# A perceiver layer on one core: the key-side queries of the later pairs turned once and dealt out by ScalarE, the second pair's loads held back, and the first products in another order

## The chip, the core and the metric

The kernel runs on one core of one Trainium2 chip. The metric is the device time of one execution in microseconds; the median of three runs before the change is 295.79 us (295.11 to 296.79). The profile is of one further execution, whose own time is given below.

## What is computed

A block takes x (8 sequences of 64 rows, 512 wide) and a context of 8 x 1601 rows, 512 wide. Three steps each add to x: attention of x on the context, an attention with a sigmoid in place of the softmax, and a feed-forward layer of 8 experts of which each row takes one. All of it is in float32. The change lies in the first step, whose reference is:

```python
qp = einsum('bsd,de->bse', layernorm(x), Wq) + bq
kp = einsum('bsd,de->bse', ctx, Wk) + bk
vp = einsum('bsd,de->bse', ctx, Wv) + bv
logits = einsum('bqe,bke->bqk', qp, kp) / sqrt(512)
x = x + einsum('bqk,bke->bqe', softmax(logits), vp)
```

## The kernel before

The keys are never made. The logits are (q Wk^T) ctx^T plus a term that is the same along a row, and the attention output is (p ctx) Wv. So each row's query is multiplied by Wk^T once ("key product", `keyed`, L308), scored against the raw context, and the context itself is summed with the probabilities.

The 512 rows of x are four tiles of 128, which are four pairs p = 0 to 3 of sequences. Each pair's context, two sequences of 1601 rows, comes in three groups of 512 rows and a tail of 65 (`load_group`, L205), one slab per group and sequence. There are twelve slabs in all; the weights use them too, and a load has to wait until a slab's last reader is done.

For the scores the context must lie with its 512 columns along the partitions. VectorE turns it in 32x32 blocks (`turn_group`, L231), which leaves four 32-row bands a = 0 to 3 of context rows; a T block holds one quarter q of the columns for one sequence and is made of three pieces and a tail. There are five T buffers, which the exponentials L share. A score matmul (`scores`, L363) takes 32 rows of R and 32 rows of T, so R must hold each 32 values of a query in all four bands. Before the change that is done in three steps: GpSimd writes q Wk^T four times over (`spread`, L335: four copies), TensorE turns the sixteen 128x128 blocks of that (`fill_queries`, L354: "turns" in what follows are such transposes, done as matmuls with an identity), and ScalarE copies them into R in four copies of 128x512. R has one buffer.

The stages of the first step, by pair: scores (`scores`, [...]four quarters), softmax (`softmax`, L376: maxima on VectorE, five exponentials on ScalarE), turns of the exponentials with a copy to SBUF on ScalarE (`chances`, L409, giving pt), sums over the context (`attend`, L418), division (`divided`, L430, giving acs), a turn of acs (`turned_sums`, L435) and the product with Wv (`project`, L440), which goes to x one pair later. Between them stand the later steps of earlier pairs: norm and turn of x, the products with aWq, aWk and aWv, alignment, sums, output (aWo), and for the pair before that the gate of the experts (`gate_parts` L690, whose copy `shares` at L700 TensorE needs for `gate`, L703).

TensorE's order is the order of the program text throughout (a manual schedule, L253). In the opening stretch VectorE and ScalarE follow the text too (L296, L876); elsewhere a scheduler orders them. [...] SyncE issues the loads of x, weights and context; GpSimd issues seven loads of constants (L886 to L892: bv, lnw, lnb, gwT, gq, gk, bo) and later blank rows and scattered rows. Instructions that are marked `keep_in_program_order` stay in the text's order on their engine.

The opening runs like this: normalise tile 0, turn it, multiply by Wq (`project_q`, L279), key product of tile 0 (L877); then turn tiles 1 to 3 (L878), multiply them by Wq (L881), turn the spread key product of tile 0 into R (L883), and start the scores. Key products of tiles 1 to 3 stand together after the first pair's softmax (L928).

Of the kernel before, what the change touches and what calls it, by code (L numbers as in the profile page):

```python
# [17 lines left out]
P = 128  # L18
B, S, D = 8, 64, 512
SK = 1601  # L20
NT = B * S // P
DC = D // P
# [14 lines left out]
def perceiver_kernel(ctx: ExitStack, tc: tile.TileContext, out: bass.AP, t: dict):  # L37
    nc = tc.nc
# [12 lines left out]
    def slab(name):  # L51
        return slabs.tile([P, DC, D], F32, tag="slab", name=name)

    def row(name):
        return rowp.tile([P, D], F32, tag="row", name=name)
# [19 lines left out]
    def load_w(name):  # L75
        w = slab(f"w_{name}")
        nc.sync.dma_start(out=w, in_=t[name])
        return w
# [23 lines left out]
    def load_b(name, n, c=None):  # L102
        if c is None:
            c = const.tile([P, n], F32, tag=name, name=f"c_{name}")
        tc.keep_in_program_order(
            nc.gpsimd.dma_start(out=c, in_=t[name].partition_broadcast(P))
        )
        return c
# [65 lines left out]
    def transposed(src, name):  # L174
        tp = bank4(f"t_{name}")
        for dc in range(DC):
            nc.tensor.transpose(tp[:, dc, :], src[:, dc * P : (dc + 1) * P], ident)
        return tp

    def projected(srcT, w, name, between=None):  # L180
        ps = bank(f"p_{name}")
        for dc in range(DC):
            if dc == DC // 2 and between is not None:
                between()
            nc.tensor.matmul(  # L185
                ps, lhsT=srcT[:, dc, :], rhs=w[:, dc, :],
                start=(dc == 0), stop=(dc == DC - 1),
            )
        return ps
# [29 lines left out]
    cxs = {}  # L219
    for g in (3, 0, 1, 2):  # L220
        cxs[0, g] = load_group(0, g)
    wv = load_w("xWv")


    NB = D // 32
    WIDTH = (416, 416, 385, 384)
# [1 line left out]
    def block_tile(p, q, b2):  # L228
        return blkp.tile([P, 4, 416], F32, tag="blk", name=f"T_{p}_{q}_{b2}")
# [41 lines left out]
    def turn_x(i, xn):  # L271
        tp = transposed(xn, f"xn{i}")
        step = 2 if i == 0 else DC
        for dc in range(0, DC, step):
            nc.scalar.copy(  # L275
                xnT[:, dc : dc + step, i * P : (i + 1) * P], tp[:, dc : dc + step, :]
            )
# [27 lines left out]

    qks = {}

    def keyed(p):  # L308

        cols = slice(p * P, (p + 1) * P)  # L310
        ps = projected(qpT[:, :, cols], wkT, f"qk{p}")
        qks[p] = row(f"qk{p}")
        nc.scalar.copy(qks[p], ps)  # L313

    def biased():

        ps = bank("qb")
        for ec in range(DC):
            for p in range(NT):
                nc.tensor.matmul(  # L320
                    ps[32 * p : 32 * p + 32, :P],
                    lhsT=bk[:, ec : ec + 1].to_broadcast([P, 32]),
                    rhs=qpT[:, ec, p * P : (p + 1) * P],
                    start=(ec == 0), stop=(ec == DC - 1),
                )
        qbT = rowp.tile([P, P], F32, tag="row", name="qbT")
        nc.scalar.copy(qbT, ps[:, :P])
        return qbT
# [6 lines left out]
    def spread(p):  # L335

        qk = qks.pop(p)
        got = []
        for b0 in range(0, NB, 4):
            q4 = rowp.tile([P, 4, 4, 32], F32, tag="row", name=f"q4_{p}_{b0}")  # L340
            nc.gpsimd.tensor_copy(  # L341
                q4,
                qk[:, 32 * b0 : 32 * b0 + 128].rearrange(
                    "p (b d) -> p b d", d=32
                ).unsqueeze(2).to_broadcast([P, 4, 4, 32]),
            )
            got.append(q4)
        return got
# [5 lines left out]
    def fill_queries(p, R, q4s, half):  # L354
        for b0 in range(8 * half, 8 * half + 8, 4):
            tp = bank4(f"rt_{p}_{b0}")
            for j in range(4):
                nc.tensor.transpose(
                    tp[:, j, :], q4s[b0 // 4][:, j, :, :].rearrange("p a d -> p (a d)"), ident
                )  # L360
            nc.scalar.copy(R[:, b0 : b0 + 4, :], tp)

    def scores(p, q, R, sc, Ts, js=range(4)):  # L363
        for j in js:
# [53 lines left out]
    def attend(p, g, pt, ac):  # L418
        cx = cxs.pop((p, g))
        nch, m = extent(g)  # L420
        for j in range(nch):
            for b2 in range(2):
                r = b2 * S
                rhs = cx[b2][:, j, :] if g < 3 else cx[b2][:m, :]
                nc.tensor.matmul(  # L425
                    ac[r : r + S, :], lhsT=pt[:m, j, r : r + S], rhs=rhs,
                    start=(g == 0 and j == 0), stop=(g == 3),
                )

    def divided(p, ac, r):  # L430
        acs = row(f"acs_{p}")
        nc.vector.tensor_scalar(acs, ac, r, None, ALU.mult)
        return acs
# [431 lines left out]
    def load_pair(p):  # L865
        for g in range(4):
            cxs[p, g] = load_group(p, g)

    def quarter(p, q):
        return [blocks(p, q, b2) for b2 in range(2)]  # L870

    def do(*steps):
        for f, i in steps:
            f(i)

    with tc.manual_schedule(engines={mybir.EngineType.Activation}):  # L876
        keyed(0)  # L877
        for i in range(1, NT):  # L878
            turn_x(i, later[i - 1])
    q4s = spread(0)  # L880
    project_q(1, NT - 1, [bank(f"qp1_{ec}") for ec in range(DC)])  # L881
    R = queries(0)
    fill_queries(0, R, q4s, 0)  # L883
    fill_queries(0, R, q4s, 1)
    qbT = biased()
    bv = load_b("xbv", D, row("c_xbv"))  # L886
    lnw = load_late("lnw", [P, DC])
    lnb = load_late("lnb", [P, DC])
# [3 lines left out]
    bo = load_b("bo", D)  # L892
    for i in range(NT):
        nc.gpsimd.tensor_tensor(xs[i], xs[i], bv, ALU.add)
    Ts = [first[0, 0], first[0, 1]]
    load_pair(1)
    awq, awk, awv, awo = (load_w(n) for n in ("aWq", "aWk", "aWv", "aWo"))
    for p in range(NT):
        i = p - 2
        if 0 < p < NT - 1:  # L900
            q4s = spread(p + 1)
        sc = [bank(f"sc_{p}_{a}") for a in range(4)]
        for q in range(4):
            if p == 0 and q == 0:
                nTs = [first[1, 0], first[1, 1]]
            elif p == 0 and q == 1:
                nTs = [first[2, 0], blocks(0, 2, 1)]
            else:
                nTs = quarter(p, q + 1) if q < 3 else None
            if i >= 0 and q == 3:  # L910
                scores(p, q, R, sc, Ts, range(3))
                do((back, i))
                scores(p, q, R, sc, Ts, (3,))
            else:
                scores(p, q, R, sc, Ts)
            Ts = nTs
            if p == 0 and q == 0:
                unturned(qbT)
            if i >= 0 and q < 3:
                do(((split, align, sums)[q], i))  # L920
        L, r = softmax(p, sc)
        pts = []

        def chance():
            pts.append(chances(p, len(pts), L))

        if p == 0:
            for k in range(1, NT):  # L928
                keyed(k)
                if k == 1:  # L930
                    q4s = spread(1)
            tables()
        else:
            do((at_turn, p - 1))
            if i >= 0:
                do((output, i))
        if p + 1 < NT:
            R = queries(p + 1)
            if p == 0:
                chance()  # L940
                fill_queries(1, R, q4s, 0)
            elif p == 1:
                fill_queries(2, R, q4s, 0)
                do((at_out, 0))
                chance()
            else:
                do((at_out, p - 1))
                fill_queries(p + 1, R, q4s, 0)
                chance()
            fill_queries(p + 1, R, q4s, 1)  # L950
        else:
            at_out(p - 1, chance)
        if 0 < p < NT - 1:
            load_pair(p + 1)
        if p == 1:
            blank_rows()
        ac = bank(f"ac_{p}")
        if i >= 0:
            do((face, i))
        for g in range(4):  # L960
            if g < 3:
                chance()
            if p > 0 and g == 3:
                do((turn, p - 1))
            if i >= 0 and g == 1:
                do((gated, i))
            attend(p, g, pts[g], ac)
            if p > 0 and g == 0:
                do((norm, p - 1))
            if i >= 0 and g == 0:  # L970
                do((logits, i))
            if i >= 0 and g == 1:
                do((routed, i))
        tile_of[p]["acs"] = divided(p, ac, r)
        if 0 < p < NT - 1:
            do((unit_q, p - 1))
            Ts = quarter(p + 1, 0)
            do((unit_k, p - 1), (gates, p - 1), (values, p - 1))
        elif p == 0:
            Ts = quarter(1, 0)  # L980


    gu, dn = load_experts()
# [218 lines left out]
```

## Time and profile before

| | before |
|---|---|
| median of 3 runs | 295.79 us |
| time of the profiled execution | 295.09 us |
| span of its instructions | 293.4 us |
| granted TensorE clock, mean | 0.998 |
| TensorE busy | 279.1 us (95%) |
| VectorE busy | 159.6 us (54%) |
| ScalarE busy | 93.2 us (32%) |
| GpSimd busy | 63.9 us (22%) |
| moved by DMA | 57.71 MB, 197 GB/s over the span |

The span runs from the first to the last instruction of the program; the time also holds some 1.7 us around it. In lines of the profile, PE is TensorE's matmuls, PEld its weight loads, DVE VectorE, ACT ScalarE, POOL GpSimd and SPq SyncE's queue. A line of a timeline gives start and duration in us, then engine, source line, operation, what it writes and reads, and how many such instructions are merged; in square brackets stands the idle time before it and what ended that. A line of the waits gives who waited for whom, and the total, the number and the longest in us. Busy time of TensorE counts matmuls that run into each other, so a short wait between two of them may not show as idle; it then shows in the waits of PEld.

### The profile page before, as it was taken

The page shows a single profiled execution, that of the slowest core. Times are in us where ns is not written, and L with a number is a line of the kernel's source. Part 1 is how long each engine was busy: PE and PEld are TensorE (multiplying, and loading weights), DVE is VectorE, ACT ScalarE, POOL GpSimd, SP SyncE. Part 2 cuts the span into 40 slices and gives each one's busy share as a digit, 9 for nine tenths or more (in the row PEclk, how much of TensorE's full clock was granted, in tenths as well). Part 3 has the DMA queues.
Part 4 walks back from the last instruction along what each step waited for, and adds up shares of the span by engine and source line. Part 5 has one row for each costly group of instructions (what it writes and reads, how often), then busy time and mean ns, then how long its engine had stood idle before and what let it go on. Part 6 is the DMA issues. An engine that isn't in the chain of part 4 may idle for free. (4 is left out here: it accounts for less than half of the span.)

```text
span 293.4 us, 6477 instructions
## 1 busy us (share of the span) xinstructions
PE 279.1 (95%) x2661; PEld 138.3 (47%) x2661; DVE 159.6 (54%) x414; ACT 93.2 (32%) x203; POOL 63.9 (22%) x110
## 2 busy tenths in 40 slices
PE   5689999999999999999999999999999999999991
PEld 5555664633554244655534465534454455343320
DVE  2554487336853477956667794453372466374140
ACT  3221403620037131326714143652425434130110
POOL 4055400600081002500220310022050032413301
PEclk9999999999999999999999999999999999999999
DMA  6999980189974993000199401959991200523401
GB/s 185 348 414 396 344 330 1 32 347 416 386 275 163 359 417 122 4 3 0 29 395 369 142 2 26 370 188 329 376 376 61 74 0 2 158 92 117 175 3 43
DMA packets 20288, 57.71 MB, mean 197 GB/s; under 512 B 2274, under 2 KB 10514, under 8 KB 16544
## 3 DMA queue, kind: packets, MB, share of 16 engines
q1 hardware_dynamic: 17568, 50.37, 47.5%
q0 software_dynamic: 2400, 6.89, 6.3%
q8 instruction: 23, 0.38, 0.5%
q14 instruction: 9, 0.07, 0.1%
q10 hardware_dynamic: 288, 0.00, 0.1%
HBM read 50.94 MB, written 6.84 MB: 197 GB/s over the span
## 5 line engine op out<-in xcount | busy, mean ns | idle before, releaser
L233 DVE STREAM_TRANSPOSE T<-cx 128x512 f32<-128x512 f32 x96 | 61.9, 681 | 25.1 <-DMA cx<-in_ctx_dram 19.4
L369 PE MATMUL sc<-T,R 32*64 32x416 f32 (+2 forms) x1024 | 49.9, 501 | 0.1
L425 PE MATMUL ac<-cx,pt 128*64 128x512 f32 x192 | 43.8, 599 | 0.0
L369 PEld LDWEIGHTS sc<-T,R 32*64 32x64 f32 x1024 | 26.5, 131 | 17.6 <-issue 6.8
L425 PEld LDWEIGHTS ac<-cx,pt 128*64 128x64 f32 x192 | 12.7, 136 | 22.1 <-issue 21.2
L1010 PE MATMUL gu<-wgu,xeT 128*32 128x512 f32 x192 | 22.9, 597 | 0.0
L501 POOL TENSOR_TENSOR gm_k<-qn_k,c_gk 128x512 f32<-128x512 f32 x4 | 5.1, 1284 | 61.4 <-DVE qn_k L496 61.4
L185 PE MATMUL p_qk<-w_xWkT,qpT 128*128 128x512 f32 x32 | 14.2, 598 | 2.9 <-DMA w_xWkT<-in_xWkT_dram 2.9
L464 POOL TENSOR_TENSOR x<-x,c_bo 128x512 f32<-128x512 f32 x4 | 5.1, 1268 | 53.6 <-DVE xh L463 53.6
L341 POOL COPY q<-qk 128x512 f32<-128x512 f32 x16 | 9.0, 615 | 34.0 <-ACT qk L313 34.0
L284 PE MATMUL qp<-xnT,w_xWq 128*128 128x128 f32 (+1 forms) x64 | 14.4, 384 | 1.3 <-ACT xnT L275 1.3
L185 PE MATMUL p_q<-w_aWq,xhT 128*128 128x512 f32 x32 | 14.8, 605 | 0.1
L185 PE MATMUL p_k<-w_aWk,xhT 128*128 128x512 f32 x32 | 14.7, 595 | 0.0
L185 PE MATMUL p_po<-w_xWv,acT 128*128 128x512 f32 x32 | 14.7, 595 | 0.0
L380 DVE TENSOR_REDUCE mx<-sc 128x1 f32<-128x416 f32 (+2 forms) x16 | 8.1, 567 | 11.9 <-PE sc L369 11.9
L185 PE MATMUL p_o<-w_aWo,cT 128*128 128x512 f32 x32 | 14.5, 596 | 0.0
L185 PE MATMUL p_v<-w_aWv,xvT 128*128 128x512 f32 x32 | 14.4, 592 | 0.0
L415 ACT COPY pt<-pp 128x512 f32<-128x512 f32 (+1 forms) x16 | 8.2, 515 | 17.5 <-PE pp L413 15.8
L284 PEld LDWEIGHTS qp<-xnT,w_xWq 128*128 128x128 f32 x64 | 9.7, 191 | 5.7 <-ACT xnT L275 1.8
L1045 PE MATMUL y<-wd,hT 128*32 128x512 f32 x96 | 11.5, 596 | 0.6 <-DVE hT L1037 0.6
L185 PEld LDWEIGHTS p_qk<-w_xWkT,qpT 128*128 128x128 f32 x32 | 5.8, 190 | 10.5 <-issue 7.4
L1020 DVE TENSOR_TENSOR h<-gu,h 128x256 f32<-128x256 f32 x6 | 2.5, 424 | 14.0 <-ACT h L1019 14.0
(198 smaller groups left out, 387.6 us busy)
## 6 DMA issues: line engine op xcount, KB each, us to landing
cx<-in_ctx_dram SPq DMA_DIRECT2D x24, 1024.0 KB, 10.1
wgu<-in_wgT_dram SPq DMA_DIRECT2D x8, 512.0 KB, 9.2
wgu<-in_wuT_dram SPq DMA_DIRECT2D x8, 512.0 KB, 10.0
wd<-in_wdT_dram SPq DMA_DIRECT2D x8, 512.0 KB, 8.4
rd<-blank POOLq DMA_DIRECT2D x6, 258.0 KB, 4.8
in<-rd SPq DMA_DIRECT2D x6, 258.0 KB, 5.0
xd<-blank POOLq DMA_DIRECT2D x6, 256.0 KB, 4.8
in<-xd SPq DMA_DIRECT2D x6, 256.0 KB, 7.2
```

The source lines that it names most:

```text
L185: nc.tensor.matmul(ps, lhsT=srcT[:, dc, :], rhs=w[:, dc, :], start=(dc == 0), stop=(dc == DC - 1),)
L233: nc.vector.transpose(T[:, :, 128 * g : 128 * g + 128].rearrange("p b (c k) -> p b c k", k=32), cxs[p, g][b2][:, :, 128 * q : 128 * q + 12 ...
L284: nc.tensor.matmul(ps[ec][:, : n * P], lhsT=wq[:, dc, ec * P : (ec + 1) * P], rhs=xnT[:, dc, cols], start=(dc == 0), stop=(dc == DC - 1),)
L341: nc.gpsimd.tensor_copy(q4, qk[:, 32 * b0 : 32 * b0 + 128].rearrange("p (b d) -> p b d", d=32).unsqueeze(2).to_broadcast([P, 4, 4, 32]),)
L369: nc.tensor.matmul(sc[a][r : r + S, : WIDTH[a]], lhsT=R[32 * a : 32 * a + 32, b, r : r + S], rhs=Ts[b2][32 * a : 32 * a + 32, j, : WIDTH[a ...
L380: nc.vector.tensor_reduce(mx[:, a : a + 1], sc[a][:, : WIDTH[a]], AX.X, ALU.max)
L415: nc.scalar.copy(pt[:m, :nch, :], tp[:m, :nch, :])
L425: nc.tensor.matmul(ac[r : r + S, :], lhsT=pt[:m, j, r : r + S], rhs=rhs, start=(g == 0 and j == 0), stop=(g == 3),)
L464: nc.gpsimd.tensor_tensor(xs[i], xs[i], bo, ALU.add)
L501: nc.gpsimd.tensor_tensor(heads(gm), heads(qn), gb.unsqueeze(1).to_broadcast([P, H, HD]), ALU.mult)
L1010: nc.tensor.matmul(ps[c, :], lhsT=xTs[k][:, dc, c], rhs=ffw[e][0][:, dc, :], start=(dc == 0), stop=(dc == DC - 1),)
L1045: nc.tensor.matmul(y[c, :], lhsT=hT[:, ic, c], rhs=ffw[e][1][:, ic, :], start=(ic == 0), stop=(ic == IC - 1),)
```

## The change

It has four parts.

- The first products. The key product of tile 0 takes a `between` argument: after two of its four matmuls the turns of tiles 1 to 3 are put, with ScalarE's copies of them; its other two matmuls follow, and the copy of the product follows on ScalarE.
- Held loads. Two slabs are written by a one-column copy on GpSimd that reads the last column of qpT, ahead of the seven constant loads on that queue; the second pair's first loads can have those slabs only after that. The load of Wv (`wv`) goes from ahead of the second pair's loads on SyncE's queue to behind them. As only ten slabs are in use by then, the second pair's first four loads get the slabs of Wq, xnT and the two held ones; its last two get those of the first pair's first group. Before, they waited for those of WkT and qpT, which now go to aWo and the third pair's first load.
- Turned and dealt. For pairs 1 to 3, `turn_queries` turns q Wk^T itself in four blocks, and `deal_queries` copies from PSUM to R in 16 copies of 32 partitions x 512, four for each band, put between the sums over the context. `spread` and `fill_queries` stay for pair 0 alone. The key product of tile 3 goes to the second pair's turn, after that of acs.
- Orders by hand. VectorE follows the text from the first pair's softmax to the second pair's second quarter: T blocks of quarters 0 and 1 of the second pair by group, the third group's two for quarter 0 ahead of `divided`, the two for quarter 1 behind it. ScalarE follows the text from each softmax to the last deal.

The diff, with context lines cut:

```diff
-    wv = load_w("xWv")
...
-    def keyed(p):
+    def keyed(p, between=None):
...
-        ps = projected(qpT[:, :, cols], wkT, f"qk{p}")
+        ps = projected(qpT[:, :, cols], wkT, f"qk{p}", between)
...
+    def turn_queries(p):
+
+        return transposed(qks.pop(p), f"rt_{p}")
+
+    def deal_queries(R, tp, a):
+
+        for j in range(4):
+            nc.scalar.copy(R[32 * a : 32 * a + 32, j::4, :], tp[32 * j : 32 * j + 32, :, :])
...
-        keyed(0)
-        for i in range(1, NT):
-            turn_x(i, later[i - 1])
+        def turn_later():
+            for i in range(1, NT):
+                turn_x(i, later[i - 1])
+
+        keyed(0, turn_later)
...
+    for k in range(2):
+        tc.keep_in_program_order(
+            nc.gpsimd.tensor_copy(slab(f"held{k}")[:, 0, 0:1], qpT[:, DC - 1, NT * P - 1 :])
+        )
     bv = load_b("xbv", D, row("c_xbv"))
...
+    def turn_second(g, qs=range(2)):
+        for b2 in range(2):
+            for q in qs:
+                turn_group(second[q, b2], 1, q, b2, g)
+
     Ts = [first[0, 0], first[0, 1]]
     load_pair(1)
+    wv = load_w("xWv")
     awq, awk, awv, awo = (load_w(n) for n in ("aWq", "aWk", "aWv", "aWo"))
     for p in range(NT):
         i = p - 2
-        if 0 < p < NT - 1:
-            q4s = spread(p + 1)
...
+            elif p == 1 and q == 0:
+                nTs = [second[1, 0], second[1, 1]]
...
+                if p == 1 and q == 1:
+                    turns.__exit__(None, None, None)
...
+        if p > 0:
+            do((at_turn, p - 1))
         L, r = softmax(p, sc)
         pts = []
+        if p == 0:
+            turns = tc.manual_schedule(engines={mybir.EngineType.DVE})
+            turns.__enter__()
+            second = {(q, b2): block_tile(1, q, b2) for q in range(2) for b2 in range(2)}
+            for g in (0, 3, 1):
+                turn_second(g)
+        acts = ExitStack()
+        if p < NT - 1:
+            acts.enter_context(tc.manual_schedule(engines={mybir.EngineType.Activation}))
...
         if p == 0:
             for k in range(1, NT):
-                keyed(k)
-                if k == 1:
-                    q4s = spread(1)
+                if k < NT - 1:
+                    keyed(k)
+            turned_qk = turn_queries(1)
+            R = queries(1)
             tables()
         else:
-            do((at_turn, p - 1))
             if i >= 0:
                 do((output, i))
-        if p + 1 < NT:
+        if p == 0:
+            chance()
+        elif p + 1 < NT:
             R = queries(p + 1)
-            if p == 0:
-                chance()
-                fill_queries(1, R, q4s, 0)
-            elif p == 1:
-                fill_queries(2, R, q4s, 0)
-                do((at_out, 0))
-                chance()
-            else:
-                do((at_out, p - 1))
-                fill_queries(p + 1, R, q4s, 0)
-                chance()
-            fill_queries(p + 1, R, q4s, 1)
+            if p == 1:
+                keyed(NT - 1)
+            do((at_out, p - 1))
+            chance()
+            turned_qk = turn_queries(p + 1)
...
             attend(p, g, pts[g], ac)
+            if p < NT - 1 and g < 3:
+                deal_queries(R, turned_qk, g)
+                if p == 0 and g == 2:
+                    deal_queries(R, turned_qk, 3)
...
+        if p == 0:
+            turn_second(2, (0,))
         tile_of[p]["acs"] = divided(p, ac, r)
+        if p == 0:
+            turn_second(2, (1,))
         if 0 < p < NT - 1:
             do((unit_q, p - 1))
+            deal_queries(R, turned_qk, 3)
+        acts.close()
+        if 0 < p < NT - 1:
             Ts = quarter(p + 1, 0)
             do((unit_k, p - 1), (gates, p - 1), (values, p - 1))
         elif p == 0:
-            Ts = quarter(1, 0)
+            Ts = [second[0, 0], second[0, 1]]
```

## The prediction

> **What bounds the kernel now.** I read the page's first part, then the timelines of TensorE, VectorE and ScalarE stage by stage, then the waits of two stretches.
>
> ```profile
> PE 279.1 (95%) x2661; PEld 138.3 (47%) x2661; DVE 159.6 (54%) x414; ACT 93.2 (32%) x203; POOL 63.9 (22%) x110
> ```
> TensorE is busy in 279.1 of 293.4 us. It takes its work in program order, so a microsecond is saved only where one of its instructions goes or one of its waits goes. The chain of waits holds only the last store and tells nothing here. The waits from 10 to 37 us:
>
> ```profile
> PE p_qk L185 <- DMA w_xWkT<-in_xWkT_dram: 2.9, 1, 2.9
> ...
> PE qp L284 <- ACT xnT L275: 0.8, 1, 0.8
> PEld sc L369 <- DVE T L233: 0.8, 1, 0.8
> ```
> Three stops of TensorE: for wkT, for the copies of turned x, and for the first scores' second context block. From 44 to 85 us another, inside a stretch that the page counts as busy, because matmuls run into each other:
>
> ```profile
> PEld sc L369 <- DVE T L240: 0.9, 2, 0.7
> ```
> The timelines of TensorE give the work that the change touches:
>
> ```profile
> 45.84 10.57 PE L185 MATMUL p_qk<-w_xWkT,qpT 128*128 128x512 f32 x24
> ...
> 56.86 1.91 PE L358 MATMUL rt<-ident,q 128*128 128x128 f32 x16
> ...
> 59.14 3.65 PE L425 MATMUL ac<-cx,pt 128*64 128x512 f32 x16
> ...
> 71.59 12.24 PE L369 MATMUL sc<-T,R 32*64 32x416 f32 x256
> ```
> Three q Wk^T take 10.41 us from start to next start, 3.47 each; 16 turns take 1.75. The second pair's scores start at 71.59 and their matmuls come 0.35 us per eight, so 256 should take 11.2; VectorE's timeline shows why they take 12.2:
>
> ```profile
> 74.73 1.90 DVE L233 STREAM_TRANSPOSE T<-cx 128x512 f32<-128x512 f32 x3 [2.24 <-PE sc L369]
> 76.55 0.27 DVE L240 STREAM_TRANSPOSE T<-tail 96x128 f32<-96x128 f32 x1
> ...
> 80.50 0.27 DVE L240 STREAM_TRANSPOSE T<-tail 96x128 f32<-96x128 f32 x1
> ```
> One T block (three pieces and a tail) costs 2.0 us from start to start. The last is done at 80.77, and the last quarter of scores, which could start at 80.02, waits for it.
>
> [...]
>
> ```profile
> 57.55 2.05 ACT L361 COPY R<-rt 128x512 f32<-128x512 f32 x4
> ```
> about 0.49 apart. [...] first-context transposes begin on landings at 18.55, 21.02, 23.52 (2.49 apart), then, after GpSimd's constants were issued at 20.13 to 24.08, at 26.84, 29.66 and 32.85 (3.11 apart). [...]
>
> **The change, part by part** (order of instructions as built).
>
> 1. *First products.* wkT still lands at 13.56. Then come two of four key products, the twelve turns, and the other two. TensorE spends the same 5.0 us, but ScalarE's three copies (1.57) now lie under the last two products (1.7) instead of before the second projection. Removed: the 0.83 wait. The key product is copied after them, some 1.1 us later; GpSimd's spread (2.26) then ends near 21.5 and is needed near 29, so nothing shows. **−0.83.**
>
> 2. *Held loads.* The two held copies wait on GpSimd for the last qpT, near 29.8. Queued behind them are seven constant loads and the four additions to x. Of these gwT is needed first, near 52, and x near 83; landing took 7.4 us, so both are in by about 43. Without the constants the last three first-context loads come at the 2.49 pace: the last lands 9.33 − 7.47 = 1.9 us earlier, at 31.0, its transpose (0.65) is done at 31.7, and R, 0.83 earlier, is there at 31.7. The wait of 0.8 goes; what is next late is R itself. **−0.8** (nothing if the landing gains under 1 us). wv moves on SyncE's queue behind the second pair, to near 61.5, and lands before 70; it is needed near 83.
>
> 3. *Turns, first pair.* Scores end 1.63 earlier, at 44.2. Before, from there to the first context product: 13.30. After: two key products 6.94; a wait for the copy of the first, which stands behind the five exponentials on ScalarE (those end at 52.6 − 1.6, the copy 0.5 later), 0.4; four turns 0.44; gs 0.27; two turns of L 1.03; a wait of 0.25 for pt, since the 16 turns that covered its copy are gone. Sum 9.3, but 3.47 is only put off to the second pair. 13.30 − 9.3 − 3.47 = **−0.5.** Context products start at 53.5 and end 12.45 later, at 65.9.
>
> 4. *Deals.* 16 copies of 32x512 on ScalarE where 4 of 128x512 were. No row before shows 32 partitions with a change of partition; [...] Below that, nothing is gained; above, every 0.1 costs 0.8 here. The last eight follow pt of the tail (ready at 61.95): 61.95 + 8 x 0.49 = 65.9, just when scores start, and their waits are per copy, so **0.**
>
> 5. *Second pair's last loads.* They take the slabs of the first pair's first group: issued near 57.2 and 57.6, when its products end. Before, two such loads issued at 56.44 and 56.86 had their transposes at 61.37 and 65.10, so 4.9 and 8.7 after the first issue. After: 62.1 and 65.9. T of the second is done at 66.5 at worst, needed at 65.9. Between 0 and 0.6; as it overlaps the next term I take **0** and keep the end for the range.
>
> 6. *VectorE's order.* The fixed order puts two transposes behind the division of acs, which waits for the last context product. From there: 0.15 start, 0.65 acs, 2 x 0.6, four T blocks at 2.0 = 10.0 us. Before, it was 80.77 − 71.6 = 9.2. The last quarter of scores waits for it in both. **+0.85.** This wait grows.
>
> 7. *Second pair.* From scores' end to the context products: 7.20 before (83.76 to 90.96). After: turns of acs 0.5, the deferred key product 3.47, the projection 3.5, L 0.5, four turns 0.44, L 0.53 = 8.94. 8.94 − 3.47 − 7.20 = **−1.73**, in which the 0.22 wait for L goes too, as 7.5 us now lie over five of exponentials. aWo and the third pair's first load now wait on SyncE for that key product (near 83 and 85.5); the load lands near 91, and xh behind it on VectorE is ready near 93, needed at 99: 0.
>
> 8. *Third pair.* Before, 137.76 to 140.91: 3.15. After 1.9. But four deals now stand before ScalarE's square roots and so before the copy of shares, for which TensorE stops. Counted from the end of the projection: pt copied by 2.5, deals 1.95, table 1.28, roots 0.5, shares 0.3 = 6.6, and TensorE asks at 6.35: 0.26. **−1.0.** The last four deals delay sq_k by 0.35 to 0.8; the turn of k comes about 3 us after qn_k, so 0.
>
> Twelve spread copies on GpSimd (0.6 each) go; they were on no path. Sum: −0.83 − 0.8 − 0.5 + 0.85 − 1.73 − 1.0 = −4.0 us. The span goes from 293.4 to 289.4, the profiled execution from 295.09 to 291.1. The median shown, 295.79, is 0.7 above that execution; I keep the difference: 291.8.
>
> **The rivals.**
>
> *The covers run out* (parts 2, 5 and 6). If the first context is bound by its own bytes, the 1.63 of parts 1 and 2 goes back into the wait for T; and if the pair of late loads is in 0.8 after TensorE asks for it (a little past the end of part 5), acs and the ten microseconds of VectorE behind it start that much later. For it: in the DMA row the 40 slices read 9 from 7 to 37 us. Against: the 2.49 pace before GpSimd's loads. −4.0 + 1.63 + 0.8 = −1.6: 294.2, between faster and no change.
>
> *Dealt copies are dear* (slower). If moving 32 rows to other partitions costs x per copy, the first pair loses 8 (x − 0.49) and the third 4 (x − 0.48). The gain of 4.0 is eaten at 0.49 + 4.0/12 = 0.82 us. At 1.2, 8.5 are lost: 300.3. For it: no such row in the profile. [...]
>
> *More is gained*: the late loads land early, shares wait for nothing, the short waits of part 3 (0.65) are covered, and half of part 6 (0.4) is: −4.0 − 0.26 − 0.65 − 0.4 = −5.3: 290.5.
>
> That the change does something else is excluded for the turns: the built order has 36 fewer.
>
> **How the numbers follow.** Forecast 0.62, covers run out 0.20, more gained 0.10, dear copies 0.08. A measurement can tell about 0.5% from no change, 1.5 us: faster is under 294.3. The forecast and the gain lie there, and half of the covers' case (0.10): 0.82; same 0.10; slower 0.08. The range leaves out the dear copies and the ends of the others: 289.9 to 294.6. The forecast's own is 290.6 to 293.
>
> **What would show it.** Right: the second projection starts near 18.5 with no wait for xnT; the first 64 score matmuls take 3.0 us, not 3.97; context products start near 53.5; the second pair's scores take over 13 us, with a wait for the last T; a deal's copy takes 0.5 apart; shares stop TensorE for a quarter microsecond. Wrong: copies of R over 0.8, scores of the second pair held at their start by a landing, or new waits after 150 us, where I expect the old order shifted by 4.

## The result and the profile after

| | before | after |
|---|---|---|
| median of 20 runs each | 295.27 us | 294.02 us (292.08 to 297.11) |
| ratio of times | | 0.9946, interval 0.9925 to 0.9967 |
| time and span of the profiled execution | 295.09, 293.4 us | 295.13, 293.4 us |
| granted TensorE clock in it, mean | 0.998 | 0.988 |

The medians differ by 1.3 us where 4.0 were forecast; the time lies near the upper end of the stated range (289.9 to 294.6). Medians, here and below, are of all executions, while the ratios leave out the slow ones, over 1.5% above the fastest of their kernel. The instructions that were to go have gone: the page of the changed kernel shows 1.6 us less of TensorE, although a stretch at half clock (below) adds some 1.7 to it, and the dealt copies as a row of their own (busy us, mean ns, idle before it).

```profile
PE 277.5 (95%) x2625; PEld 136.9 (47%) x2625; DVE 159.5 (54%) x414; ACT 114.6 (39%) x239; POOL 57.5 (20%) x100
...
L369 ACT COPY R<-t_rt 32x512 f32<-32x512 f32 x48 | 27.7, 577 | 0.8
```

A later profile of the same kernel had a time of 292.49 us, so two executions can be set beside the forecast. The table gives starts on TensorE in us; the forecast column is what the parts on record add up to.

| | before | forecast | after, first profile | after, second profile |
|---|---|---|---|---|
| end of first pair's scores | 45.84 | 44.2 | 46.76 | 43.80 |
| first pair's context products | 59.14 | 53.5 | 56.06 | 53.10 |
| second pair's scores | 71.59 | 65.9 | 68.52 | 65.56 |
| second pair's context products | 90.96 | 88.0 | 90.62 | 87.50 |
| third pair's scores | 114.86 | 111.9 | 115.03 | 112.63 |
| third pair's context products | 140.91 | 136.7 | 139.85 | 137.46 |

Two steps miss. In the opening the first profile is 2.6 us behind the forecast, and the second is not. From the second pair's context products to the third pair's scores both are late: 24.4 and 25.1 us where before had 23.9. All other steps are within 0.5 of the forecast in both.

*The opening.* TensorE's timeline of the changed kernel, first profile:

```profile
30.67 0.91 PE L377 MATMUL sc<-T,R 32*64 32x416 f32 x2
32.84 4.71 PE L377 MATMUL sc<-T,R 32*64 32x416 f32 x62 [1.26 <-DVE T L232]
```

The scores can start at 30.67, a microsecond sooner than forecast. That is mostly luck: wkT was there at 12.68 and not at 13.56 as before, which nothing in the change explains. Then TensorE stands until 32.84 for a T block. VectorE's timeline shows why; the forecast had the last landing at 31.0:

```profile
25.71 1.30 DVE L232 STREAM_TRANSPOSE T<-cx 128x512 f32<-128x512 f32 x2 [0.59 <-DMA cx<-in_ctx_dram]
28.19 1.90 DVE L232 STREAM_TRANSPOSE T<-cx 128x512 f32<-128x512 f32 x3 [1.18 <-DMA cx<-in_ctx_dram]
32.08 1.30 DVE L232 STREAM_TRANSPOSE T<-cx 128x512 f32<-128x512 f32 x2 [1.99 <-DMA cx<-in_ctx_dram]
```

Five landings keep the pace of 2.49; the sixth takes 3.89. And after the wait the 62 score matmuls take 4.71 us; in runs below, behind a wait of the same kind, 62 take 3.02. The windows (busy us of PE, in brackets matmuls, then the granted clock, the DMA share and GB/s) show why:

```profile
30.00:31.00 1.00, 1.00 (x29) 1.00 1.05 332
...
33.00:34.00 1.00, 1.00 (x29) 0.94 1.00 414
34.00:35.00 1.00, 1.00 (x24) 0.50 1.00 397
35.00:36.00 1.00, 1.00 (x20) 0.50 1.02 349
36.00:37.00 1.00, 1.00 (x22) 0.50 1.00 360
37.00:38.00 1.00, 1.00 (x16) 0.86 1.04 407
```

The clock is halved for 0.12 + 3 + 0.28 = 3.4 us (0.94 and 0.86 are half clock in 0.12 and 0.28 of those slices), which costs 1.7. The DMA engines are all busy at 30 to 31, but at 332 GB/s, where the kernel before moved 420 from 30 to 32.

*The second pair.* SyncE's queue, GpSimd's and VectorE's timelines:

```profile
85.98 0.35 SPq L77 DMA_DIRECT2D w_aWo<-in_aWo_dram  x1
86.42 16.69 SPq L212 DMA_DIRECT2D cx<-in_ctx_dram  x7
```
```profile
78.99 0.56 POOL L654 DMA_DIRECT2D xd<-blank  x1 [0.26 <-POOL blank L652]
...
85.83 0.54 POOL L655 DMA_DIRECT2D rd<-blank  x1
```
```profile
97.25 0.71 DVE L232 STREAM_TRANSPOSE T<-cx 128x512 f32<-128x512 f32 x1 [6.13 <-DMA cx<-in_ctx_dram]
98.31 0.54 DVE L471 TENSOR_SCALAR xh<-x,mv_b,rs 128x512 f32<-128x512 f32 x1
...
104.11 0.36 DVE L480 TENSOR_SCALAR xhT<-t_xh,c_lnw,c_lnb 128x128 f32<-128x128 f32 x1
```

The third pair's first load, issued at 86.42, is transposed at 97.25 and not near 91: GpSimd's twelve stores of blank rows (3.16 MB) are in the DMA engines before it. From 86 to 88 us every packet (185, 0.59 MB) was of GpSimd's queue. Its transpose stands on VectorE ahead of xh (98.31; before 93.97), more transposes stand ahead of xhT, and TensorE stops for that. The waits of the changed kernel:

```profile
PE sc L377 <- DVE T L232: 1.3, 1, 1.3
PE sc L377 <- DVE T L239: 0.9, 1, 0.9
PE p_q L185 <- DVE xhT L480: 0.7, 1, 0.7
...
PE pl L716 <- ACT shares L708: 0.6, 1, 0.6
```

### The profile page after: what moved, and what is told of

Its sections match the earlier page's. It is cut to its first block, busy times and chain, and to the rows that moved or that the text cites. A ratio compares the mean times of both kernels' runs of the same rounds, so it can differ in the third digit from the quotient of the medians.

```text
span 293.4 us, 6408 instructions
## 1 busy us (share of the span) xinstructions
PE 277.5 (95%) x2625; PEld 136.9 (47%) x2625; DVE 159.5 (54%) x414; ACT 114.6 (39%) x239; POOL 57.5 (20%) x100
## 5 line engine op out<-in xcount | busy, mean ns | idle before, releaser
L377 PE MATMUL sc<-T,R 32*64 32x416 f32 (+2 forms) x1024 | 51.9, 515 | 2.1 <-DVE T L232 1.3
L377 PEld LDWEIGHTS sc<-T,R 32*64 32x64 f32 x1024 | 28.9, 134 | 18.8 <-issue 6.8
L369 ACT COPY R<-t_rt 32x512 f32<-32x512 f32 x48 | 27.7, 577 | 0.8
L185 PEld LDWEIGHTS p_q<-w_aWq,xhT 128*128 128x128 f32 x32 | 5.7, 189 | 9.7 <-issue 5.9
```

Of the source, the lines that this page charges most:

```text
L185: nc.tensor.matmul(ps, lhsT=srcT[:, dc, :], rhs=w[:, dc, :], start=(dc == 0), stop=(dc == DC - 1),)
L369: nc.scalar.copy(R[32 * a : 32 * a + 32, j::4, :], tp[32 * j : 32 * j + 32, :, :])
L377: nc.tensor.matmul(sc[a][r : r + S, : WIDTH[a]], lhsT=R[32 * a : 32 * a + 32, b, r : r + S], rhs=Ts[b2][32 * a : 32 * a + 32, j, : WIDTH[a ...
```

## The experiments

Theory: the gain is lost in the opening, because the second pair's two small tail loads reach the DMA engines together with the last load of the first context, and because the wait that this makes can halve TensorE's clock; and what the opening gains is partly given back in the second pair, to the blank-row stores. Rivals: the first context is bound by its own bytes; GpSimd's constants, issued from 28.91 us on, delay its last load; the clock falls by itself; other transfers hold the second pair. The first run with tails behind and the two of "all together" have six timed executions each, the others 16 to 22.

**Once more.** The changed kernel.

> The changed kernel once more, beside the next three on the same chip. My theory: the shortfall of 2.4 us arises in the opening and is the same in each execution: the sixth first-context transpose begins about 3.9 us after the fifth (the others 2.5 apart), the first scores wait about 2 us for it, and for some 3.5 us after that wait the granted TensorE clock is near 0.5, so the first 62 score matmuls take about 4.7 us. Rival (one odd execution): the sixth transpose stands 2.5 us behind the fifth, or the clock stays at 1.0. Time about 294.0 us, 0.995 of before.

Measured: 293.61 us, ratio 0.9942 (0.9913 to 0.9971). Half of the theory held. The sixth transpose came 2.98 after the fifth, at 30.69 (and the fourth 3.25 after the third). There was no wait and no half clock: the loss in the opening is not in each execution. But the wait for xhT was 1.4 us here. The mean clocks of the 36 timed executions of the changed kernel fall in two groups: 17 under 0.992, with a median of 294.7 us, and 19 above, with 293.0. One stretch of 3.4 us at half clock takes 0.006 off the mean (half of 3.4 in 293). Of 171 timed executions of the kernel before, 19 were under 0.992. For the kernels below this cut is not sharp: two of their traces have such a stretch at means of 0.992 and 0.993.

**Tails behind.** The part of the tail tiles that is set to zero is written later, so their loads are issued behind four others:

```diff
-    for k in range(2):
-        for b2 in range(2):
-            nc.gpsimd.memset(tails[k][b2][64:96, :], 0.0)
+    for b2 in range(2):
+        nc.gpsimd.memset(tails[0][b2][64:96, :], 0.0)
...
+    for b2 in range(2):
+        tc.keep_in_program_order(nc.gpsimd.memset(tails[1][b2][64:96, :], 0.0))
     bv = load_b("xbv", D, row("c_xbv"))
```

> The second pair's two tail loads (65 rows each) wait until the last qpT and are issued behind that pair's first four loads. My theory (their small packets slow the last first-context load, now that Wv no longer stands between): the sixth first-context transpose begins near 30.7, the scores wait under 0.4 us for it, the clock stays near 1.0 from 33 to 38, first-pair scores end near 44.5 instead of 46.8, and the time is 291.5 to 292.5, 1.5 to 2.5 below the changed kernel. Rival (the last load is late by its own bytes, as the first context is bound by them): sixth transpose at 32, time unchanged at 294. Second rival (the clock falls by itself at 34 us): sixth transpose early but scores still slow, gain under 1 us.

Measured: 292.09 us, ratio 0.9896 (0.9834 to 0.9958). VectorE's and TensorE's timelines of this run:

```profile
28.21 1.90 DVE L231 STREAM_TRANSPOSE T<-cx 128x512 f32<-128x512 f32 x3 [1.19 <-DMA cx<-in_ctx_dram]
30.68 1.30 DVE L231 STREAM_TRANSPOSE T<-cx 128x512 f32<-128x512 f32 x2 [0.57 <-DMA cx<-in_ctx_dram]
```
```profile
30.80 3.66 PE L376 MATMUL sc<-T,R 32*64 32x416 f32 x64
```

The sixth landing keeps the pace (2.47), so the first context is not bound by its own bytes, and the tails are what delays it. One trace of each kind would not show that, but all traces agree: in the six with tails behind the sixth transpose begins 2.45 to 2.49 after the fifth, in the five with the tails in their place and the constants held 2.98 to 3.89. The DMA view of 28 to 32 us has for the changed kernel (first profile) and for this run, in this order:

```profile
DMA packets 273, 1.13 MB, mean 283 GB/s; under 512 B 38, under 2 KB 38, under 8 KB 167
...
q1 hardware_dynamic: 273, 1.13, 98.9%
```
```profile
DMA packets 174, 1.32 MB, mean 330 GB/s; under 512 B 13, under 2 KB 13, under 8 KB 13
...
q1 hardware_dynamic: 174, 1.32, 88.5%
```

Of 2 to 8 KB there are 167 - 38 = 129 packets against none: the two tails are 130 rows of 2 KB. All packets are of SyncE's queue (q1), so the constants, which GpSimd issues, moved nothing in that time and are not the cause. Why packets that stand behind a load on its own queue delay it, no run here shows. Scores of the first pair end at 43.67, which is 3.1 us earlier than in the changed kernel's first profile and 0.1 earlier than in its second. The interval of the time overlaps the changed kernel's. But the wait for xhT grew to 1.9, and there the clock halved:

```profile
101.00:102.00 1.00, 0.00 (x0) 1.00 1.03 434
102.00:103.00 1.00, 0.42 (x1) 0.58 1.06 451
103.00:104.00 1.00, 1.00 (x2) 0.50 0.95 401
104.00:105.00 1.00, 1.00 (x2) 0.50 1.03 434
105.00:106.00 1.00, 1.00 (x3) 0.71 0.99 418
```

**The wait filled.** TensorE gets useless work ahead of the first scores:

```diff
     qbT = biased()
+    idle_turns(18)
```

> Eighteen TensorE transposes of no use stand ahead of the first scores, about 2 us, the length of the wait. The T they wait for is as late as in the changed kernel. If the wait itself brings the clock down: the clock stays near 1.0 from 33 to 38, the first 62 score matmuls take about 2.9 instead of 4.7 us, and the time is 1.3 to 1.9 below the changed kernel. If the clock falls for another reason: 0.5 all the same, and the time is the same or a little above.

Measured: 293.83 us, ratio 0.9943 (0.9921 to 0.9966). The sixth transpose was as late as in the changed kernel (32.19, 3.74 after the fifth), the clock stayed at 1.0, and the scores ended at 45.18:

```profile
29.94 2.19 PE L118 MATMUL idle<-ident 128*128 128x128 f32 x18
32.06 3.92 PE L377 MATMUL sc<-T,R 32*64 32x416 f32 x64
```

So in this execution nearly the same landing cost 1.6 less. The time does not differ from the changed kernel's: an execution whose landing is early pays up to 2 us for the filling. One trace of each kind doesn't prove that the idle time halves the clock. The timed executions speak for it too: with the wait filled 4 of 22 have a mean clock under 0.992, in the changed kernel 17 of 36. With longer waits, below, there are more: 18 of 22 with the constants early, 55 of 88 in the four runs with blank rows near 105 us. And in every trace here with a half clock before 285 us, it begins during a wait of TensorE or at most 1.1 us after one.

**Constants early.** The two held copies stand behind the seven constant loads:

```diff
-    for k in range(2):
-        tc.keep_in_program_order(
-            nc.gpsimd.tensor_copy(slab(f"held{k}")[:, 0, 0:1], qpT[:, DC - 1, NT * P - 1 :])
-        )
     bv = load_b("xbv", D, row("c_xbv"))
...
     bo = load_b("bo", D)
+    for k in range(2):
+        tc.keep_in_program_order(
+            nc.gpsimd.tensor_copy(slab(f"held{k}")[:, 0, 0:1], qpT[:, DC - 1, NT * P - 1 :])
+        )
```

> The two held copies stand behind the seven constant loads on GpSimd instead of ahead of them, so that the constants are loaded from about 20 us as before the change; the rest is the changed kernel. If holding the constants was worth something: the fourth to sixth first-context transposes begin about 0.3 to 1 us later each, the sixth at 33 to 34, time 0.5 to 1.5 above the changed kernel. If the tails alone set the last landing: sixth at 32 to 32.8, time within 0.5 of the changed kernel.

Measured: 296.40 us, ratio 0.9995 (0.9964 to 1.0027). The last three transposes began 2.67, 3.24 and 4.51 us after the one ahead, the sixth at 34.26; the scores waited 2.2 us and then had the half clock. Holding the constants is worth about what the whole change gained.

**Blank rows later.** Twice: behind the second pair's acs (near 105 us), then behind the third pair's gate copies (near 118 us). The tile is made from acs, so that the stores can't go earlier. The diff has the second place; for the first, the call stands behind the second pair's last deal.

```diff
-        blank = blkp.tile([P, D + 4], F32, tag="blk", name="blank")
-        nc.gpsimd.memset(blank[:, :D], 0.0)
+        blank = rowp.tile([P, D + 4], F32, tag="row", name="blank")
+        acs = tile_of[1]["acs"]
+        nc.gpsimd.tensor_tensor(blank[:, :D], acs, acs, ALU.subtract)
...
                 do(((split, align, sums)[q], i))
+                if p == 2 and q == 1:
+                    with tc.manual_schedule(engines={mybir.EngineType.Pool}):
+                        blank_rows()
...
-        if p == 1:
-            blank_rows()
```

> The changed kernel with GpSimd's twelve blank-row stores (3.16 MB) put behind the second pair's acs, near 106 us, where the traces show no other transfers; their tile is made of acs minus acs and has a buffer of the rows. My theory: in the second pair these stores stand between the third pair's first loads and their landing, and TensorE waits at p_q because VectorE's queue holds xhT behind the transposes of those loads. Without them the transposes of the third pair's first two loads begin some 4 us earlier, the wait at p_q (0.7 to 1.9 us in three executions of the changed kernel and of the one with tails behind) is gone, and the time is 0.5 to 1.5 below the changed kernel. Rival (the loads are late because aWo stands ahead of them on SyncE's queue): the wait stays within 0.3 of what it was and the time is the same.

Measured, near 105 us: 298.07 us, ratio 1.0087 (1.0063 to 1.0112), slower. The wait for xhT was gone, as expected, and another had come. The expectation was wrong in that no other transfers run there: in the first profile of the changed kernel the DMA engines moved 375 to 451 GB/s from 104 to 112 us. GpSimd's, VectorE's and TensorE's timelines:

```profile
112.77 0.54 POOL L655 DMA_DIRECT2D xd<-blank  x1 [3.30 <-DMA xd<-blank]
...
116.34 1.28 POOL L509 TENSOR_TENSOR gm_k<-qn_k,c_gk 128x512 f32<-128x512 f32 x1
```
```profile
117.66 0.69 DVE L513 TENSOR_REDUCE gate_k<-gm_k 128x16 f32<-128x512 f32 x1 [4.17 <-POOL gm_k L509]
...
121.64 0.65 DVE L528 COPY kT<-t_k 128x512 f32<-128x512 f32 x1
```
```profile
122.44 1.55 PE L542 MATMUL al<-qT,kT 32*64 32x64 f32 x60 [2.94 <-DVE kT L528]
```

Issuing stopped for 3.30 us until an earlier store was done. The gate multiplication stood behind the stores, kT behind the gate on VectorE, and TensorE stood 2.9 us; from 121.5 to 128.3 us, 6.8 in all, the clock was at half. Tails behind and these stores together:

> Tails behind and blank rows late together. My theory: the first run with tails behind kept only 2.0 of the 3.1 us that its opening gained, because the wait at p_q grew by what the opening gave; with the stores away both stay: scores of the first pair end near 43.7, the third pair's scores start near 111.5 (before 114.9), no wait at p_q, the clock at 1.0 to 280 us, time 289.5 to 290.8, that is the 4 us below before that were forecast, or more. Rival (something else holds the second pair): time 291.5 to 292.5, as with tails behind alone.

Measured: 296.32 us, ratio 1.0002 (0.9979 to 1.0025), with the same stop at `al` (3.5 us). Third pair's scores started at 110.77 (111.5 expected). So the loss of time lies behind that, where the experiment's own new wait stands.

> The changed kernel with the blank-row stores behind the third pair's gate copies on GpSimd, near 120 us, instead of at 79 us; nothing of GpSimd's is queued behind them that is wanted before 135 us. When they stood at 104 us the wait at p_q was gone, but the gate multiplications stood behind them on GpSimd, VectorE's copy kT behind those, and TensorE waited 2.9 us at al and then ran at half its clock. My theory: now neither wait is there; third pair's scores start some 0.5 to 1.2 us earlier counted from the second pair's first sums than in the changed kernel, time 0.5 to 1.5 below it, 292.5 to 293.5. Rival (the stores cost their time wherever they stand): a new wait over 1 us between 120 and 150 us, time as the changed kernel's or above.

Measured, near 118 us: 292.98 us, ratio 0.9935 (0.9910 to 0.9960). No wait for xhT and none at `al` above 0.2; from the second pair's context products to the third pair's scores 23.69 us, against 24.4 and 25.1. With the stores late no trace of the seven has that wait. With the stores in their place three traces have it (0.7, 1.4 and 1.9 us), but two have not: the wait filled and the constants early, with 23.9 and 23.7 us for that stage. So the stores make the wait, in some executions and not in all. In the time the gain is small, and its interval overlaps the changed kernel's.

**VectorE's order, and deals behind shares.** Both on top of tails behind and stores near 105:

```diff
...
-            turn_second(2, (0,))
+            third = block_tile(1, 2, 0)
+            for k in (0, 3, 1):
+                turn_group(third, 1, 2, 0, k)
+            turn_group(second[0, 0], 1, 0, 0, 2)
+            turn_group(second[1, 0], 1, 1, 0, 2)
+            turn_group(third, 1, 2, 0, 2)
+            turn_group(second[0, 1], 1, 0, 1, 2)
         tile_of[p]["acs"] = divided(p, ac, r)
         if p == 0:
-            turn_second(2, (1,))
+            turn_group(second[1, 1], 1, 1, 1, 2)
...
+            if i >= 0 and p < NT - 1:
+                for k in ((), (0,), (1, 2), ())[g]:
+                    deal_queries(R, turned_qk, k)
```

> As the run before, and VectorE's order changed: the third quarter's first T block, and the third group's pieces that the first of the two late loads allows, stand ahead of the wait for the second load. 2.6 of the ten microseconds of VectorE behind that load move ahead of it. My theory (the wait of the last quarter is VectorE's chain behind the late load): scores of the second pair take about 12.0 to 12.3 us instead of 13.2, time 0.8 to 1.2 below the run before. Rival (the blocks' buffers, or the landing, bind): scores still 13 us, time the same.

> As the run before, and in the third pair the first deals stand behind the copy of shares on ScalarE (deals at the second and third sums instead of the first three). My theory: the wait for shares (0.55) goes and the first sums are followed by the gate without a stop; time 0.4 to 0.7 below the run before, near 288.5, the fastest of all. Rival (the table load and roots alone hold shares up): wait above 0.3, no difference of time, or the moved deals are late for the fourth pair's scores and the time is up by 0.5 or more.

Measured: 295.64 us, ratio 0.9975 (0.9945 to 1.0006), with VectorE's order; 295.28 us, 0.9965 (0.9937 to 0.9994), with both. The second pair's scores take 12.82 and 12.88 us instead of 13.26, less than half of what was expected. VectorE now waits elsewhere, for a T buffer that the first quarter of scores still reads (run with both):

```profile
66.63 0.70 DVE L231 STREAM_TRANSPOSE T<-cx 128x512 f32<-128x512 f32 x1
69.28 1.90 DVE L231 STREAM_TRANSPOSE T<-cx 128x512 f32<-128x512 f32 x3 [1.95 <-PE sc L376]
```

So the chain behind the late load held the last quarter up, and behind what was moved the rival (buffers) binds next. Shares no longer stop TensorE; that part came out as expected in the trace. The times alone don't separate these runs from the one before them.

**All together,** with the stores near 118 us; first tails and stores, then all four.

> Tails behind, and the stores near 120 us. My theory: both losses are gone, no TensorE wait over 1 us and no half clock from 15 to 285 us; first-pair scores end near 43.5, third pair's scores start near 110.8, fourth pair's sums 4 us before those of the changed kernel's first profile; 289.5 to 291, so the 4 us of the forecast are there. Rival: another wait opens and the time stays at 292.

> The same with VectorE's order and the deals behind shares. These two took 0.4 us (second pair's scores 13.26 to 12.88; a block's buffer then bound) and 0.4 us (no wait for shares) in the trace of the run that had them. Time 0.6 to 1.0 below the run before: 288.7 to 290.2, the fastest of all.

Measured: 291.66 us, ratio 0.9882 (0.9843 to 0.9922), a little over the 291 that were expected at most; why is not shown. In the profiled execution (292.17) the expected waits were gone, but it had a half clock from 13.2 to 16.6 us, after a wait of 1.9 for wkT. With all four: 290.80 us, ratio 0.9836 (0.9801 to 0.9870): the fastest, faster than the changed kernel too, whose interval lies wholly above. What TensorE still waits for longest between 20 and 285 us:

```profile
PE sc L376 <- DVE T L231: 1.3, 1, 1.3
PE y L1099 <- DVE hT L1091: 0.6, 1, 0.6
...
```

The scores could start at 29.67, and the sixth transpose begins at 31.16, 2.49 after the fifth; after this wait of 1.3 the clock was at half again for 3.4 us. The first context is the bound here, though not at its best pace: the third transpose came 3.81 after the second. In three of the other five traces with tails behind it was 3.0 to 3.3; the cause stays open.

**First products alone,** in the kernel before:

```diff
-        keyed(0)
-        for i in range(1, NT):
-            turn_x(i, later[i - 1])
+        def turn_later():
+            for i in range(1, NT):
+                turn_x(i, later[i - 1])
+
+        keyed(0, turn_later)
```

> The kernel before with the order of the first products alone. My forecast gave this part 0.83. If that holds by itself: no wait for xnT, time 0.8 below before. Theory: R comes earlier, but the first scores wait for the last first-context block, whose landing the constants on GpSimd and the second pair's loads set; the 0.83 goes into that wait, the scores start within 0.3 of where they did, and the time is within 0.5 of before, or above it where the longer wait brings the half clock.

Measured: 296.13 us, ratio 1.0031 (1.0009 to 1.0053): slower, if anything. The wait for xnT was gone, but the trace had a half clock elsewhere, from 13.1 to 16.6 us, in and after a wait for wkT:

```profile
13.60 3.42 PE L185 MATMUL p_qk<-w_xWkT,qpT 128*128 128x512 f32 x4 [2.68 <-DMA w_xWkT<-in_xWkT_dram]
...
33.06 3.60 PE L369 MATMUL sc<-T,R 32*64 32x416 f32 x64
```
```profile
13.00:14.00 1.00, 0.40 (x1) 0.43 (x2) 0.93 (x5) 0.00 (x0) 0.00 (x0) 0.57 0.97 258
14.00:15.00 1.00, 1.00 (x2) 0.41 (x2) 0.53 (x1) 0.00 (x0) 0.00 (x0) 0.50 1.01 293
```

The first two key products took 3.42 us there, in the changed kernel 1.96. So R was not early in this trace: the scores start at 33.06 (before 32.66), without a stop, and end at 45.86 (before 45.84). The sixth transpose begins at 32.87, so an earlier R would have met a wait for T, as the theory says; this trace doesn't test it. The timed executions decide it: of 22, 11 have a mean clock of 0.992 or more, and their median is 295.7 us, against 295.2 for the kernel before. The other 11 are half of all, where the kernel before had one in nine. By itself this part gains nothing.

## Why the prediction was wrong, by its steps

**Part 2 failed.** The forecast was: "Without the constants the last three first-context loads come at the 2.49 pace", and "The wait of 0.8 goes; what is next late is R itself". In the first profile two of the three came at that pace. The third met the second pair's tails and took 3.89. The tails' loads were issued at 15.5 in the changed kernel, directly behind the last first-context load; in the kernel before, Wv (1 MB) stood between. I followed the moved Wv to its own landing and not what closed up behind it. So the landing gained 0.8 us (32.85 to 32.08) and not 1.9, and the forecast's own condition, "nothing if the landing gains under 1 us", came true. That the tails delay the landing is shown by the runs with tails behind; that Wv's place is what kept them off before is read from the queue's order and was not tried alone. I had put the late landings of before on GpSimd's constants, which was an estimate. With the constants early the last three landings are late again (2.67, 3.24 and 4.51 us), but in the first profile every packet from 28 to 32 us was of SyncE's queue (q1 above), so the constants don't explain this delay.

**A cost was missing: the half clock.** I priced a wait at its length. In the first profile a gap of 1.3 us in the busy time cost 1.7 more. Up to 285 us, each stretch measured here has 3.4 us at half clock or twice that. Gaps of 1.2 and 1.4 passed without it in other traces, and 2.9 for wkT in the kernel before. Why nearly the same gap sometimes costs this and sometimes doesn't, no run here shows.

**Part 1** was right in its mechanism: no wait for xnT in either profile, and from the first key product to the second projection 4.82 and 5.28 us where before had 5.83. By itself it gained nothing in time; that the landing takes the gain away is argued, not shown.

**Part 3** held: 9.30 us to the context products in both profiles, 9.3 forecast. **Part 4** was mis-sized: 0.585 apart and 577 ns each, not 0.49, which was an estimate from the 0.49 between copies of 128x512. The last eight ended 0.7 after the second pair's scores had started (69.2 against 68.5), where the forecast had them end with the start; it cost nothing, as the waits are per copy. **Part 5** held to the tenth: issued at 59.74, transposes at 64.61 and 68.42, 4.9 and 8.7 later. **Part 6** held in the main: +1.2 in the first profile, +1.0 in the second, for +0.85; VectorE ran from the second late load to the last T without a stop, as the forecast had it.

**Part 7** held up to the context products (8.76 us for 8.94). Its last sentence failed: "the load lands near 91, and xh behind it on VectorE is ready near 93, needed at 99: 0." The load's issue, 86.42, was near the forecast one; the forecast didn't ask what would stand in the DMA engines then. The blank-row stores were in the trace of before, at 81 to 88 us, behind the load that they now precede (issued at 71.26 then). The cost was 0.5 in one profile and 1.2 in the other; two traces of other runs have none.

**Part 8** was right in its sign: 1.84 us for 1.9 to the context products; shares stop TensorE by 0.55 and not 0.26 (the terms given add up to 6.53, which makes it 0.18). The dearer deals account for 4 x 0.1 of that.

Sum: 291.1 was forecast for the profiled execution. The second profile is 1.4 above it: 0.4 less in the opening, 1.2 more in the second pair, and 0.6 more between the third and fourth pair's context products (+0.85 for +0.26, shares the largest part). The first is 4.0 above it, of which 2.6 lie in the opening, 0.5 in the second pair and 0.6 there. Among the timed executions with a mean clock of 0.992 or more, 152 of the kernel before have a median of 295.2 us and the 19 of the changed kernel 293.0, a gain of 2.2. The other executions of the changed kernel, about half, lie 1.6 us higher.

*The rivals.* "The covers run out" gave 294.2, and the time, 294.02, is near that. Its wait for T did come, but not by its cause: the first context is not bound by its own bytes in the changed kernel, and the late pair of loads was on time. That the time lies in the stated range is thus luck. Dear copies are refuted (0.585 against 0.82 to break even).

## What to carry to other kernels

When a load is moved on a queue, ask what closes up behind the gap it leaves: two loads of 130 KB, in rows of 2 KB, delayed one of 1 MB by 0.5 to 1.4 us here. When a load is made to wait for a later reader, it can fall behind another engine's burst that it used to precede, so its landing has to be checked against that burst: it cost TensorE 0.5 and 1.2 us here. And a new wait of TensorE can cost more than its length: one of 1.3 us was followed by 3.4 us at half clock here, 1.7 us more, and one of 1.4 by none. Look at the granted clock after it.

## What was not expected of the hardware

- The half clock in or after short waits: before 285 us, 3.4 us in eight traces, 6.8 in two, with gaps of 1.3 to 3.8 us, and not with each gap of such a length (1.4 and 2.9 passed without it).
- Two loads of 130 KB that stood behind a load of 1 MB on the same queue delayed that load by 0.5 to 1.4 us; from 28 to 32 us the constants on the other queue moved nothing.
- A copy on ScalarE of 32 partitions to others took 0.585 us from start to start, one of 128 partitions with as many elements per lane 0.49.
- GpSimd's stores of 256 KB were issued 0.53 apart, but near 105 us, with other transfers under way and eight stores issued, issuing stopped for 3.30 us until an earlier store was done, and held up the arithmetic behind it.
